# A two-layer model on one core: the first layer's prologue rearranged (first batch's convolutions among the row work, expert routing next, token sends beside the step sizes, order written out)

## The chip, the cores and the metric

The kernel runs on one core of one Trainium2 chip. A core has five engines that work at the same time, each through its own queue of instructions, strictly in order: TensorE (PE, matrix products and transposes; loading its weights shows as PEld), VectorE (DVE), ScalarE (ACT), GpSimd (POOL) and SyncE (SP, which only issues transfers). An engine that reaches an instruction whose inputs are not there waits, and everything behind it in its queue waits too. The metric is device time of one execution in microseconds; the times given are medians of several executions, and the profile is of one further execution.

## What is computed

Two layers over 8 batches of 512 tokens of width 256. Each layer is `x = x + attention(norm(x)) + experts(norm(x))`. In the first layer, which the change touches, "attention" is a state-space scan and "experts" a routed feed-forward net:

```python
xn = _layernorm(x)
# scan: in two directions, 8 heads, chunks of 128 tokens
zxbcdt = xn @ in_proj_w.T                     # z | x,B,C | dt
xBC = silu(causal_conv(xBC, conv_w, 4 taps))
dt = softplus(dt + dt_bias);  A = -exp(A_log)
Y = ssd(x * dt, A * dt, B, C, chunk=128)      # forward and backward direction
y = shift(Y + x * D); y = y_fw + y_bw + x * (x @ fc_D_w.T + D)
out = rmsnorm(y * silu(z)) @ out_proj_w.T
# experts: each token goes to the one expert of highest probability
probs = softmax(xn @ Wr + br); gate, idx = max(probs), argmax(probs)
y = gate * (relu(xn @ W1[idx] + b1[idx]) @ W2[idx] + b2[idx])
```

The second layer is softmax attention with 16 heads and a top-2 routed net of seven experts. Its code is the same in both kernels.

## The kernel before

**Stages of the first layer.** (1) *Row work*, `norm_and_project`: for each of the 8 batches, mean and variance (lines 134, 135), a Newton reciprocal root (164 to 174), the normalised rows `xn` (140), their transpose `xT` (147, 148), and a small product that gives 16 step-size inputs and 8 expert scores per token (`pp`, 152, copied to `proj`, 156). `xT` is also written to memory (`xtd`, 366) for later. (2) *Step sizes* in `steps()`: the softplus as a series in VectorE instructions (392 to 406), from which `dt` and `da` come. (3) *The first batch's convolutions*: for each of eight channel blocks a product `pj` (746) from `xT` and `w_in`, an ACT instruction that starts `cv` (755), three taps on VectorE (759), a tanh on ACT (763) and one more VectorE instruction (764). (4) *The opening*: decays, the first chunk's segment sums, the skip term (`skip`, 782 to 791; `start`, 809 and 816), the exponent rows for all chunks (`edges`). (5) *The chunk loop*: 64 chunks, eight per batch (four positions, two directions). Chunk n's matrix `mt` is multiplied by the masked `cb` (`weigh`, 970) and used in `inside` (`yd`, 976), then come `before` (`yoff`, 994), `behind` (`sp`, 1002) and the segment sums of the chunk after (`seg`, 938). In between are pieces of the neighbouring batches' convolutions and outputs.

**What fills the loop.** Each chunk calls `fill(1)` four times (five times for the first two of a batch; two more calls through `fill(2)` in the last eight chunks). A fill advances one generator by one step: first `route0()` (softmax, arg-max, ranks, slot numbers `slot0`, then 32 sends of token rows to their expert slots `xd0` with GpSimd's indirect transfers, line 459, two per step), then `blocks()` (39 blocks of 128 slots through the experts: gathers of weights, line 524; `xdT_ps` 540, `h_ps` 559, `y_ps` 577), and when both are used up `late()` (per batch: add the experts' rows, second normalisation, transpose, router product; lines 628 to 666). Block 0 reads `xd0`, so it waits for all 32 sends. `late` for a batch waits until the scan's output of that batch is done.

**Who sets the order.** Stages 1 to 4 stand outside the written-out region: there a planner places the instructions of each engine by its own estimates. From the chunk loop on (`tc.manual_schedule`) the program order is the order of every queue.

**Transfers of the prologue.** The slots `xd0` are first cleared with zeros from ACT's queue (`clear`, line 121, one eighth per batch). A batch's rows `u` are loaded through two buffers, so the load for batch b waits until the rows of batch b-2 are normalised.

Of the kernel before, what the change touches and what calls it, by code (L numbers as in the profile page):

```python
# [17 lines left out]
P = 128  # L18
# [35 lines left out]
def bc(ap, axis, shape):  # L54

    return ap.unsqueeze(axis).to_broadcast(shape)
# [3 lines left out]
def tile_kernel(ctx: ExitStack, tc: tile.TileContext, t, out: bass.AP):  # L60
# [63 lines left out]
        )  # L124


    def norm_and_project(x_of, xn, xT_of, w_proj, n_proj, proj, pool, bank):

        for b in range(B):
            x = x_of(b)  # L130
            mv = pool.tile([P, TPB, 2], FP, name="mv", tag="mv")
            for c in range(TPB):
                st = pool.tile([P, 6], FP, name="st", tag="st", bufs=4)
                V.bn_stats(st, x[:, c, :])
                V.bn_aggr(mv[:, c, :], st)
            ve = pool.tile([P, TPB], FP, name="ve", tag="ve")
            V.tensor_scalar(ve, mv[:, :, 1], EPS, None, ALU.add)
            rs = rsqrt(pool, ve, [P, TPB])
            for c in range(TPB):
                V.tensor_scalar(  # L140
                    xn[:, b * TPB + c, :], x[:, c, :], mv[:, c, 0:1], rs[:, c : c + 1], ALU.subtract, ALU.mult
                )
            xT = xT_of(b)
            for k in range(KC):
                tp = bank("tp", [P, S], 0)
                for c in range(TPB):
                    T.transpose(tp[:, c * P : (c + 1) * P], xn[:, b * TPB + c, k * P : (k + 1) * P], ident)
                A.copy(xT[:, k, :], tp)
            pp = bank("pp", [P, TPB, n_proj], 1)
            for c in range(TPB):  # L150
                for k in range(KC):
                    T.matmul(
                        pp[:, c, :], xT[:, k, c * P : (c + 1) * P], w_proj[:, k, :],
                        start=(k == 0), stop=(k == KC - 1),
                    )
            V.tensor_copy(proj[:, b * TPB : (b + 1) * TPB, :], pp)

    def rsqrt(pool, v, shape):

# [199 lines left out]
    proj = r0b.tile([P, NTILE, 2 * NH + NE], FP, name="proj0", tag="proj0")  # L359

    def steps():
        pool, big = r0p, r0b
        xTs = {}

        def keep(b):
            Y.dma_start(out=xtd[b], in_=xTs[b])

        def x_of(b):
            if b:
                keep(b - 1)  # L370
            if b >= 2:
                ask(b)

            n = NBLK // B + 1
            clear(xd0, NBLK * P, b * n, min(NBLK, (b + 1) * n))
            if b == 3:
                Y.dma_start(out=w_in, in_=t["w_in"])
            if b == 5:
                Y.dma_start(out=w_out, in_=t["w_out"])
            return us[b]  # L380

        def xT_of(b):
            xTs[b] = m2.tile([P, KC, S], FP, name="xT", tag="xT")
            return xTs[b]

        norm_and_project(x_of, xn, xT_of, w_small, 2 * NH + NE, proj, pool, bank)
        keep(B - 1)

        v, u, z, z2 = (row(n).rearrange("p (t e) -> p t e", e=2 * NH) for n in ("sp_v", "sp_u", "sp_z", "sp_z2"))
# [12 lines left out]
        V.tensor_tensor(acc, acc, z, ALU.mult)  # L404
        V.tensor_scalar(acc, acc, 2.0, None, ALU.mult)
        V.scalar_tensor_tensor(dt.rearrange(f2), v.rearrange(f2), 0.0, acc.rearrange(f2), ALU.max, ALU.add)
        ea = big.tile([P, 2 * NH], FP, name="ea", tag="ea")
        A.activation(ea, a_log, AF.Exp)
        V.tensor_scalar(ea, ea, -1.0, None, ALU.mult)
        for d in range(2):  # L410
            of = slice(d * NH, (d + 1) * NH)
            V.tensor_tensor(da[:, d], dt[:, :, of], bc(ea[:, of], 1, [P, NTILE, NH]), ALU.mult)


    def route0():

        big = r0b

# [23 lines left out]
        V.tensor_copy(slot0, slots_of(big, oh, rank, "a"))  # L442
# [12 lines left out]
        yield  # L455

        sent = []
        for i in range(NTILE):
            one = G.indirect_dma_start(
                out=xd0, out_offset=bass.IndirectOffsetOnAxis(ap=slot0[:, i : i + 1], axis=0),  # L460
                in_=xn[:, i, :], in_offset=None, bounds_check=NBLK * P - 1, oob_is_err=False,
            )
            for other in sent:
                tc.declare_no_dep(one.ins, other.ins, reason="rows go to slots of their own")
            sent.append(one)
            if i % 2:
                yield

    def decays():
# [26 lines left out]
        A.activation(e8, ct, AF.Exp)  # L496
        Y.dma_start(out=exd.rearrange("g p l -> p g l"), in_=e8)

    steps()
    l1c = tl = w_r = rb = w_q = w_o = w_uk = w_uv = w_kv = band = slot1 = iota_n = proj1 = vt0 = qk0 = r1b = noop = None  # L500
    tls = ExitStack()
    for k in range(HC):
        V.tensor_scalar(w_out[:, k, :], w_out[:, k, :], norm_w[:, k : k + 1], None, ALU.mult)

    with ExitStack() as es:
        p1, p2, psum = m1, m2, mp
        H3 = [P, NH, P]
# [518 lines left out]


        first = batch[0]
        first.load()
# [12 lines left out]
        decays()  # L1042
        chunk[0].prepare()
        chunk[0].segments()
        chunk[0].cross(range(NH))
        chunk[1].prepare()
        chunk[0].pairs(first)
        chunk[0].weigh()
        edges()
        batch[1].load()  # L1050
        e2 = None

        with tc.manual_schedule(engines=ENGINES):

            def others(n):

# [36 lines left out]
            for n in range(N):  # L1093
# [683 lines left out]
```

## Time and profile before

| what | us |
|---|---|
| median of 3 runs (2068.0 to 2072.36) | 2070.32 |
| the profiled execution, its own time | 2064.15 |
| its span | 2062.4 |
| first chunk's `yd` | 130.72 |
| slot numbers ready, first send | 148.4, 148.90 |
| last send starts | 203.71 |
| first block's first product | 213.02 |
| last chunk's `yd` | 1061.81 |
| last output product of the scan ends | 1095.7 |

PE is busy 1838.8 us (89% of the span), VectorE 1435.8 (70%), ACT 1178.1 (57%), GpSimd 627.8 (30%). A timeline line gives the start and the length in us, the engine, the line of the kernel, the operation, what it writes and reads, and how many instructions are merged in it; a bracket gives the idle time of the engine before it and what ended it. A line of the table by stretches gives the stretch, its length, and then busy time and (in brackets) instruction count of PE, PEld, VectorE, ACT and GpSimd, the TensorE clock granted (1.00 is full), the share of the DMA engines' time and the rate.

### The profile page before, as it was taken

What the parts mean: (1) busy time and instruction counts of PE and PEld (TensorE: products, weight loads), DVE (VectorE), ACT (ScalarE), POOL (GpSimd) and SP (SyncE); (2) the same over time, 40 slices, a digit from 0 to 9 for tenths busy, and PEclk for the clock granted to TensorE, in tenths of its full rate; (3) what the DMA queues carried; (4) which work ended last, traced back from release to release, by engine and by line L of the source; (5) the groups of instructions that cost most, each with busy time, mean ns of one, the idle gap of its engine ahead of it and who ended that gap; (6) DMA issues with size and microseconds to landing.
All of it is one profiled execution on the core that took longest, in us unless ns stands there. A gap on an engine that the chain in (4) does not pass through costs nothing. (4 is left out here: it accounts for less than half of the span.)

```text
span 2062.4 us, 33308 instructions
## 1 busy us (share of the span) xinstructions
PE 1838.8 (89%) x11760; PEld 1235.9 (60%) x11760; DVE 1435.8 (70%) x3311; ACT 1178.1 (57%) x2536; POOL 627.8 (30%) x572
## 2 busy tenths in 40 slices
PE   5666999999999999987776998899999999999987
PEld 5333676767677677744544544466666666666654
DVE  4684766667485665668665787567777877787785
ACT  2243454545354454545433667577777877787776
POOL 0048644546454454555430035300000000000030
PEclk9877999999999999998776899799999999999998
DMA  7113654655455465543542254322231221213170
GB/s 265 62 49 113 212 196 159 210 186 194 148 186 196 156 218 187 159 130 101 169 138 96 98 183 150 108 80 72 68 93 45 87 72 55 81 54 104 34 162 14
DMA packets 150439, 262.34 MB, mean 127 GB/s; under 512 B 22361, under 2 KB 107212, under 8 KB 138368
## 3 DMA queue, kind: packets, MB, share of 16 engines
q1 hardware_dynamic: 112288, 139.62, 21.1%
q0 software_dynamic: 28512, 110.92, 17.3%
q10 hardware_dynamic: 9472, 9.67, 1.4%
q8 instruction: 93, 1.52, 0.3%
q14 instruction: 74, 0.61, 0.1%
HBM read 188.46 MB, written 76.68 MB: 129 GB/s over the span
## 5 line engine op out<-in xcount | busy, mean ns | idle before, releaser
L1476 DVE TENSOR_SCALAR s<-s_ps 128x512 f32<-128x512 f32 x512 | 318.1, 683 | 200.4 <-PE s_ps L1471 178.6
L1486 ACT ACTIVATE s<-s,ng 128x512 f32<-128x512 f32 x512 | 351.1, 727 | 14.7 <-DVE ng L1482 13.3
L1478 DVE CUSTOM_DVE_ANT_0 s<-s,band 128x512 f32<-128x512 f32 x512 | 323.0, 687 | 0.0
L1493 PE MATMUL p_ps<-ident,s 128*128 128x128 f32 x2048 | 291.7, 283 | 33.2 <-ACT pT L1494 33.2
L1494 ACT COPY pT<-p_ps 128x512 f32<-128x512 f32 x512 | 280.4, 590 | 44.6 <-PE p_ps L1493 35.5
L1493 PEld LDWEIGHTS p_ps<-ident,s 128*128 128x128 f32 x2048 | 242.6, 145 | 101.5 <-ACT pT L1494 59.8
L1281 POOL DMA_INDIRECT x<-e_yo,e_to x28 | 43.4, 1552 | 605.4 <-ACT e_yo L1280 542.6
L746 PE MATMUL pj<-xT,w_in 128*128 128x512 f32 x384 | 206.1, 664 | 14.9 <-DVE cv L759 12.2
L1471 PE MATMUL s_ps<-kT,qT 16*128 16x512 f32 x1024 | 164.6, 678 | 14.0 <-DVE s L1476 9.5
L559 PEld LDWEIGHTS h_ps<-xdT,w 128*128 128x128 f32 x1248 | 149.4, 193 | 22.3 <-issue 21.5
L559 PE MATMUL h_ps<-xdT,w 128*128 128x128 f32 x1248 | 153.0, 276 | 2.9 <-DMA w<-in_w_dram,w_idx 2.9
L759 DVE SCALAR_TENSOR_TENSOR cv<-pj,w_conv_w,cv 128x511 f32<-128x511 f32 (+2 forms) x192 | 143.1, 746 | 9.7 <-ACT cv L755 5.7
L577 PE MATMUL y_ps<-w,hT 128*128 128x256 f32 x624 | 147.3, 380 | 0.0
L922 POOL TENSOR_TENSOR au<-da,half 128x512 f32<-128x512 f32 x64 | 78.6, 1229 | 221.5 <-PE seg L938 119.8
L1502 PE MATMUL o_ps<-pT,vt 128*32 128x256 f32 x2048 | 139.9, 403 | 1.8 <-issue 1.7
L577 PEld LDWEIGHTS y_ps<-w,hT 128*128 128x128 f32 x624 | 115.9, 190 | 32.1 <-issue 18.1
L746 PEld LDWEIGHTS pj<-xT,w_in 128*128 128x128 f32 x384 | 72.7, 207 | 98.6 <-issue 89.6
L996 POOL TENSOR_TENSOR yT<-yT,ex 128x512 f32<-128x512 f32 (+1 forms) x48 | 59.2, 1233 | 226.1 <-DVE ex L995 159.2
L1262 PE MATMUL e_hp<-e_xdT,e_w 128*128 128x256 f32 x448 | 122.3, 395 | 2.2 <-ACT e_xdT L1247 0.8
L1502 PEld LDWEIGHTS o_ps<-pT,vt 128*32 128x32 f32 x2048 | 66.4, 115 | 94.1 <-issue 62.9
L1275 PE MATMUL e_yp<-e_w,e_hT 128*128 128x256 f32 x448 | 118.9, 388 | 0.1
L951 ACT ACTIVATE mt<-seg,mid 64x64 f32<-64x64 f32 x512 | 109.5, 309 | 0.8
(296 smaller groups left out, 3019.8 us busy)
## 6 DMA issues: line engine op xcount, KB each, us to landing
ex<-exd SPq DMA_DIRECT2D x96, 128.0 KB
u<-in_u_dram SPq DMA_DIRECT2D x16, 512.0 KB
xtd<-xT SPq DMA_DIRECT2D x16, 512.0 KB
fr<-fdd SPq DMA_DIRECT2D x64, 128.0 KB
xT<-xtd SPq DMA_DIRECT2D x15, 512.0 KB
od<-os SPq DMA_DIRECT2D x28, 256.0 KB
e_w<-in_ei_dram SPq DMA_DIRECT2D x7, 1024.0 KB
e_w<-in_eo_dram SPq DMA_DIRECT2D x7, 1024.0 KB
```

Source lines behind the costliest of these rows:

```text
L559: T.matmul(hp[:, i, :], w1[:, k * FF + f * P : k * FF + (f + 1) * P], xdT[:, k * P : (k + 1) * P], start=(k == 0), stop=(k == KC - 1),)
L577: T.matmul(yp, hT[f // 4][:, f % 4, :], w2[:, f * DM : (f + 1) * DM], start=(f == 0), stop=(f == FC - 1))
L746: T.matmul(pj, w_in[:, k, o * P : (o + 1) * P], self.xT[:, k, :], start=(k == 0), stop=(k == KC - 1))
L759: V.scalar_tensor_tensor(cv[:, s:], pj[:, : S - s], conv_w[:, q, 3 - s : 4 - s], cv[:, s:], ALU.mult, ALU.add)
L1262: T.matmul(hp, w1[:, k, f * P : (f + 1) * P], xdT[:, k, :], start=(k == 0), stop=(k == KC - 1))
L1471: T.matmul(sp[i], self.q[r, cols], self.k[r, :], start=True, stop=True)
L1476: V.tensor_scalar(self.p[i], sp[i], -CLAMP, CLAMP, ALU.max, ALU.min)
L1478: V.tensor_tensor_reduce(out=self.p[i], in0=self.p[i], in1=band[:, at : at + S], scale=1.0, scalar=-3.0e38, op0=ALU.mult, op1=ALU.max, acc ...
L1486: A.activation(self.p[i], self.p[i], AF.Exp, bias=self.ng[:, i : i + 1])
L1493: T.transpose(pp[:, k, :], self.p[i][:, k * P : (k + 1) * P], ident)
L1494: A.copy(pT[i][:, :, cc * P : (cc + 1) * P], pp)
L1502: T.matmul(op[32 * i : 32 * i + 32, half * 2 * P : (half + 1) * 2 * P], self.v[:, k, h * (AD + 1) : h * (AD + 1) + 32], pT[i][:, k, :], st ...
```

## The change

1. `first.x_part` and `first.bc_part` (the first batch's eight convolutions) are called from a new callback `behind(b)` after batch b's small product, two per batch from batch 2 on. Batch 0's `xT` gets a buffer of its own, and the load of `w_in` moves from batch 3 to batch 1.
2. The clears are no longer spread over the batches. After batch 4 a wide tile of zeros (`none`) is made on VectorE, from data of that batch, and four transfers from ACT's queue clear all of `xd0`, in runs of 4 KB.
3. The written-out region now begins before the routing. In it come, in this order: routing through `w_idx`, the skip term with the first 12 sends between its parts, the step sizes, tokens, decays, the first chunks' preparation, `edges`, segments, `start`, and `weigh`.
4. The softplus series takes one fused VectorE instruction per term in place of two.
5. The sends advance four per fill in place of two, and the last eight chunks fill once where they filled twice.

```diff
@@ def norm_and_project
             V.tensor_copy(proj[:, b * TPB : (b + 1) * TPB, :], pp)
+            behind(b)
@@ def steps
-            n = NBLK // B + 1
-            clear(xd0, NBLK * P, b * n, min(NBLK, (b + 1) * n))
-            if b == 3:
+            if b == 1:
                 Y.dma_start(out=w_in, in_=t["w_in"])
...
+        def behind(b):
+            for q in range(2 * b - 4, min(2 * b - 2, 2 * HC)) if b >= 2 else ():
+                part = first.x_part if q < HC else first.bc_part
+                slot(lambda: part(q % HC))
+            if b == B - 1:
+                while pending:
+                    slot()
+            if b == B // 2:
+                none = m1.tile([P, HC, S], FP, name="none", tag="z").rearrange("p k s -> p (k s)")[:, : TPB * DM]
+                V.tensor_scalar(
+                    none.rearrange("p (k d) -> p k d", d=DM), bc(zero[:, :DM], 1, [P, TPB, DM]),
+                    proj[:, b * TPB, :1], 0.0, ALU.min, ALU.max,
+                )
+                slots = xd0.rearrange("(p r) d -> p r d", p=P)
+                for lo in range(0, NBLK, 3 * TPB):
+                    n = min(3 * TPB, NBLK - lo)
+                    k = n // 3 if n % TPB else TPB
+                    A.dma_start(
+                        out=slots[:, lo : lo + n, :].rearrange("p (n k) d -> p n (k d)", k=k),
+                        in_=bc(none[:, : k * DM], 1, [P, n // k, k * DM]),
+                    )
@@ def step_sizes (was the end of steps)
-        V.tensor_scalar(acc, z2, 1.0 / 17.0, 1.0 / 15.0, ALU.mult, ALU.add)
-        for k in range(13, 0, -2):
-            V.tensor_tensor(acc, acc, z2, ALU.mult)
-            V.tensor_scalar(acc, acc, 1.0 / k, None, ALU.add)
-        V.tensor_tensor(acc, acc, z, ALU.mult)
+        V.tensor_scalar(acc, z2, 1.0 / 17.0, None, ALU.mult)
+        for k in range(15, 1, -2):
+            V.scalar_tensor_tensor(acc, acc, 1.0 / k, z2, ALU.add, ALU.mult)
+        V.scalar_tensor_tensor(acc, acc, 1.0, z, ALU.add, ALU.mult)
@@ def route0
-            if i % 2:
+            if i % 4 == 3:
                 yield
@@ before the chunk loop
-        first.load()
-        for q in range(4):
-            slot(lambda: first.x_part(q))
-        slot(), slot()
-        first.skip()()
-        first.ask(0), first.ask(1)
-        for q in range(4):
-            slot(lambda: first.bc_part(q))
-            if q == 0:
-                pending.append(first.start())
-        while pending:
-            slot()
-        first.tokens(0)(), first.tokens(3)()
-        decays()
-        chunk[0].prepare()
-        chunk[0].segments()
-        chunk[0].cross(range(NH))
-        chunk[1].prepare()
-        chunk[0].pairs(first)
-        chunk[0].weigh()
-        edges()
-        batch[1].load()
         with tc.manual_schedule(engines=ENGINES):
+            routing = route0()
+            for _ in range(6):
+                next(routing)
+            skip = first.skip()
+            next(routing)
+            skip()
+            next(routing)
+            first.ask(0), first.ask(1)
+            next(routing)
+            step_sizes()
+            for c in (0, TPB - 1):
+                first.tokens(c)()
+            decays()
+            chunk[0].prepare()
+            chunk[1].prepare()
+            edges()
+            chunk[0].segments()
+            chunk[0].pairs(first)
+            chunk[0].cross(range(NH))
+            pending.append(first.start())
+            while pending:
+                slot()
+            chunk[0].weigh()
+            batch[1].load()
...
-            rows, rest = itertools.chain(route0(), blocks()), late()
+            rows, rest = itertools.chain(routing, blocks()), late()
...
                 if n >= N - 8:
-                    fill(2)
+                    fill(1)
```

More of the change, by code (lines that the diff above doesn't have):

```diff
@@ L124, in clear, with norm_and_project @@
         )
-    def norm_and_project(x_of, xn, xT_of, w_proj, n_proj, proj, pool, bank):
+    def norm_and_project(x_of, xn, xT_of, w_proj, n_proj, proj, pool, bank, behind):
         for b in range(B):
@@ L361, in steps @@
     def steps():
-        pool, big = r0p, r0b
+        pool = r0p
         xTs = {}
@@ L382, in xT_of, with step_sizes @@
         def xT_of(b):
-            xTs[b] = m2.tile([P, KC, S], FP, name="xT", tag="xT")
+            if b == 0:
+                first.xT = xTs[b] = m2.tile([P, HC, S], FP, name="xT0", tag="yT")[:, :KC, :]
+            else:
+                xTs[b] = m2.tile([P, KC, S], FP, name="xT", tag="xT")
             return xTs[b]
-        norm_and_project(x_of, xn, xT_of, w_small, 2 * NH + NE, proj, pool, bank)
+        def behind(b):
[19 more added lines that the diff above has]
+                    )
+        norm_and_project(x_of, xn, xT_of, w_small, 2 * NH + NE, proj, pool, bank, behind)
         keep(B - 1)
+    def step_sizes():
+        big = r0b
         v, u, z, z2 = (row(n).rearrange("p (t e) -> p t e", e=2 * NH) for n in ("sp_v", "sp_u", "sp_z", "sp_z2"))
@@ L399, in steps @@
         acc = u
[L400 to L404 removed]
+        acc, z, z2, v = (a.rearrange(f2) for a in (u, z, z2, v))
+        V.tensor_scalar(acc, z2, 1.0 / 17.0, None, ALU.mult)
+        for k in range(15, 1, -2):
+            V.scalar_tensor_tensor(acc, acc, 1.0 / k, z2, ALU.add, ALU.mult)
+        V.scalar_tensor_tensor(acc, acc, 1.0, z, ALU.add, ALU.mult)
         V.tensor_scalar(acc, acc, 2.0, None, ALU.mult)
[L406 removed]
+        V.scalar_tensor_tensor(dt.rearrange(f2), v, 0.0, acc, ALU.max, ALU.add)
         ea = big.tile([P, 2 * NH], FP, name="ea", tag="ea")
@@ L497, in edges @@
         Y.dma_start(out=exd.rearrange("g p l -> p g l"), in_=e8)
-    steps()
     l1c = tl = w_r = rb = w_q = w_o = w_uk = w_uv = w_kv = band = slot1 = iota_n = proj1 = vt0 = qk0 = r1b = noop = None
     tls = ExitStack()
-    for k in range(HC):
-        V.tensor_scalar(w_out[:, k, :], w_out[:, k, :], norm_w[:, k : k + 1], None, ALU.mult)
     with ExitStack() as es:
@@ L1028, in tile_kernel @@
         first = batch[0]
+        steps()
         first.load()
-        for q in range(4):
-            slot(lambda: first.x_part(q))
-        slot(), slot()
-        first.skip()()
-        first.ask(0), first.ask(1)
-        for q in range(4):
-            slot(lambda: first.bc_part(q))
-            if q == 0:
-                pending.append(first.start())
-        while pending:
-            slot()
-        first.tokens(0)(), first.tokens(3)()
-        decays()
-        chunk[0].prepare()
-        chunk[0].segments()
-        chunk[0].cross(range(NH))
-        chunk[1].prepare()
-        chunk[0].pairs(first)
-        chunk[0].weigh()
-        edges()
-        batch[1].load()
+        for k in range(HC):
+            V.tensor_scalar(w_out[:, k, :], w_out[:, k, :], norm_w[:, k : k + 1], None, ALU.mult)
         e2 = None
         with tc.manual_schedule(engines=ENGINES):
+            routing = route0()
[22 more added lines that the diff above has]
+            batch[1].load()
             def others(n):
```

## The prediction

> **What bounds the kernel now.** First the busy time by stretches (span start, first `yd`, the first block, the last block, last output of the scan), then the timelines of single engines at these borders. Between them the layer falls into four parts.
>
> ```profile
> core 0: us, PE busy (x) PEld busy (x) DVE busy (x) ACT busy (x) POOL busy (x), PEclk, DMA share, GB/s
> 0.00:72.00 72.00, 44.51 (x190) 39.80 (x191) 33.76 (x162) 14.29 (x28) 3.30 (x20) 1.00 0.65 226
> ...
> 224.19:886.89 662.70, 649.63 (x3949) 469.31 (x3948) 436.98 (x731) 319.38 (x871) 338.08 (x293) 1.00 0.54 180
> 886.89:1095.70 208.81, 159.77 (x791) 102.13 (x790) 139.53 (x289) 89.04 (x204) 86.55 (x80) 0.82 0.42 132
> 130.72:224.19 93.47, 63.99 (x270) 35.27 (x270) 53.04 (x103) 29.70 (x79) 66.08 (x64) 0.79 0.38 129
> 72.90:130.72 57.82, 36.27 (x85) 13.50 (x84) 50.37 (x77) 24.28 (x50) 10.30 (x8) 0.78 0.11 35
> ```
>
> While blocks run beside chunks, 224.19 to 886.89 (45 chunks, 14.73 us each), PE is busy 98%: only work taken off PE would shorten that. Around it PE has gaps. In 72.9 to 130.7 VectorE is the bound (87%); in 130.7 to 224.2 six chunks run while routing and sends go by, without blocks; after 886.9 the blocks are used up and twelve chunks run beside `late`. So the change can win only by filling gaps outside the middle part, and what it moves out of one gap lands in another.
>
> ```profile
> 72.69 0.26 DVE L156 COPY proj<-pp 128x96 f32<-128x96 f32 x1 [5.33 <-PE pp L152]
> ...
> 148.41 0.18 DVE L442 CAST slot<-so_sa 128x32 int32<-128x32 f32 x1
> ```
>
> ```profile
> 148.90 1.24 POOL L459 DMA_INDIRECT xd<-xn,slot  x1 [6.92 <-DVE slot L442]
> ...
> 203.71 1.24 POOL L459 DMA_INDIRECT xd<-xn,slot  x1 [0.30 <-DMA xd<-xn,slot]
> 204.97 1.05 POOL L922 TENSOR_TENSOR au<-da,half 128x512 f32<-128x512 f32 x1
> 207.27 1.06 POOL L524 DMA_INDIRECT w<-in_w_dram,w_idx  x1 [1.25 <-DMA xd<-xn,slot]
> ```
>
> ```profile
> 130.72 1.98 PE L976 MATMUL yd<-mt,xdt 128*64 128x128 f32 x16 [4.19 <-DVE mt L970]
> ...
> 213.02 2.81 PE L559 MATMUL h_ps<-xdT,w 128*128 128x128 f32 x16 [2.87 <-DMA w<-in_w_dram,w_idx]
> ...
> 224.19 1.09 PE L976 MATMUL yd<-mt,xdt 128*64 128x128 f32 x16
> ```
>
> The reader sees that block 0 starts 8.1 us after the last send is done by GpSimd (204.95 to 213.02), and that it starts in chunk 5.
>
> **Row work with the convolutions in it: R = 96.5 instead of 72.9.** I walk the order in which the changed kernel issues on each engine, with the rows' lengths. Eight transposes take 2.1 us, sixteen small products 3.7, a convolution's product 1.98 (four records, clock 1.00) or 3.75 (cold, at 85.09), its ACT parts 0.78 and 0.63, its taps 2.3, its last VectorE part 0.6; a batch's statistics 1.8, its normalisation 1.35. Batches 0 and 1 now go through PE back to back: 10.2 to 22.3. First product to 24.3, ACT to 25.1, taps to 27.4; statistics of batches 2 and 3 to 31.0 (their `u` is issued behind two `xtd` writes, at 19.4, and lands in time); one last part, six taps, two Newton roots and two normalisations with another last part: 40.2. Here VectorE's queue holds the copy of batch 2's `proj` and then batch 3's. PE does transposes 2, half a convolution, products 2 (to 43.5), transposes 3, the other half, products 3 (to 50.0), so VectorE waits some 7 us between them. Three taps more, the root and batch 4's normalisation: 57.8; two taps and a last part: 60.5; wait for products 4: 63.4; the wide zero tile (1.0, twice the 0.43 of a 512-wide TENSOR_SCALAR), taps, batch 5: 69.6; batch 6's statistics and three scalings of `w_out`: 71.6. Batch 7's `u` can be asked only at 69.7, when the clears (5 MB at the 381 GB/s of the stretch 14 to 22 us, 13 us from 66) are moving. Before, `u` of batch 2 took 8 us through such traffic (issued 14.6, used 22.5); so it lands at 77.3, its statistics end at 79.2, and 7.3 us of queue follow plus 9.7 for transposes, products and copies of 6 and 7: R = 96.5. With no such delay it is 92; if that load took twice as long, 104.
>
> [...]
>
> **From R to the first block.** Routing on VectorE, by its rows from 73.59 to 74.92 and from 130.49 to 149.83, with PE's `both` (2.07) and an ACT exp (0.5) inside and what lies between left out: 16.3 to `slot0`, 1.3 more to `w_idx`. Before, these were shared with the first two chunks; now PE has only small products beside them. The first send goes at R + 16.6 = 113.1 against 148.9. Sends cost 1.28 each (150.44 and 158.72 on), so twelve end at R + 32. The step sizes take 15.8 (ACT 1.35, the reciprocal 3.39, eight fused instructions at 0.72, six others and `da`): `da` at R + 33.4. The fusing saves seven TENSOR_SCALAR of 0.42, 2.9 us, which are in this sum. Then GpSimd: four `xdt` (1.05 each), one `au` 1.1: R + 37.8; `seg` 1.1; the masked `cb` on VectorE at R + 39.8. `start` stands in front of `weigh` in VectorE's queue: 4 x (0.6 + 1.4) = 8.0, then `weigh` 1.5: first `yd` at R + 49.5 = 146, 15 us later than before. (In the old trace `start` was spread among the taps.)
>
> All other sends stand in chunk 0's five fills: 5 x 4 = 20. Queued on GpSimd: four sends (R + 47.5 to 52.6), two `xdt` that need `xp` behind the first `yd` (to 55), four sends (60.1), `xdd` (61.2), twelve sends (76.6). Behind them stand `au` and the weight gathers, and in PE's queue block 0's transpose stands in chunk 1, before that chunk's `cb`, `sp` and next `seg`. With the old 8.1 us, block 0 starts at R + 84.7 = 181, and chunk 2's `yd` follows 9 us later (two times 2 us of `h_ps`, `sp`, `seg`, half a `y_ps`, transposes): R + 94 = 190.5. So the chunk loop stands still some 20 us in chunk 1, with nothing beside it.
>
> **Middle and end.** Blocks start 32 us earlier (213 to 181), but in chunk 1 and not 5. The pattern of pieces is the same, shifted by four chunks: 45 chunks at 14.73, 662.7 us, bounded by PE. Then 16 chunks instead of 12 share the same `late` steps (seven batches inside, one left over in both). What does a chunk without block or `late` cost? The old end shows 11.98 between two `yd` (904.01 to 915.99), and 10.7 and 12.0 in other light ones. Going through the 16 chunks with old chunks of like content gives 252 for this part instead of 208.8, so 43 for four chunks. Bounds: 34 (8.5 each, if spreading `late` thinner hides some of it) to 50. The fill taken from the last eight chunks is in this: batch 6's `late` moves from the tail into chunk 62.
>
> Sum for the changed kernel: 96.5 + 94 + 662.7 + 251.8 + the unchanged 966.7 (2062.4 - 1095.7; order and pieces of the second layer are the same) = 2071.7 against 2062.4: +9.3. The profiled execution took 2064.15, the median of the runs is 6.2 above it; I carry the difference over: 2070.3 + 9.3 = 2079.6, predicted 2080. In short: change = R - 130.2 + (four chunks at the end) = 96.5 - 130.2 + 43.
>
> **Rivals.** (a) *Faster*: the row work hides the convolutions. Old PE and VectorE are busy only 44.5 and 33.8 of 72 us, and the convolutions bring PE 16 and VectorE 23, so room is there. It decides at R = 83 (below: faster by over 0.2%). That needs the waits at `proj` copies 2 and 3 (7 us) and batch 7's late load (4.5) to vanish together with little else. For R = 80 the time is 2063. Against it: those copies are in front of ready taps in an in-order queue. (b) *Parity*: R = 92 and 39 for the last four chunks: +1, 2071. For it: the old end has 49 us of PE gaps. (c) *The first block is later still*: PE stays cold after a 20 us stall (the clock is 0.79 there in the old stretch), VectorE's `start` doubles beside GpSimd (at 124.16 two such took 2.97 instead of 1.53), the load of `u` doubles: +10 to +20 more, 2095. (d) *It does nothing*: routing was hidden beside the first chunks, the new order only permutes. The four unmatched chunks speak against it; it falls in with (b).
>
> **How the numbers follow.** Forecast 0.55, its own range 2074 to 2089; (a) 0.16; (b) with (d) 0.16; (c) 0.13. The range takes (b), most of (a) and the lower part of (c): 2063 to 2095. Less than 0.2% (4 us) can't be told from no change by these runs. Faster 0.17, same 0.16, slower 0.67.
>
> **What would show it.** Last `proj` copy near 96; first send near 113; first `yd` near 146; a gap of some 20 us on PE in chunk 1 that ends with the gather of weights, first `h_ps` near 181; last `h_ps` some 34 us earlier than 876, and about 252 us from chunk 47's `yd` to the last output product. It is wrong if the row work ends before 85, if the sends don't hold the first block, or if the last four chunks cost much less than 10 us each.

## The result, and the profile after

The changed kernel takes 2106.2 us (median; 2098.4 to 2110.6) against 2071.3 of the kernel before on the same chip: ratio 1.0155, 95% interval 1.0122 to 1.0189; slower by some 32 us by that ratio, by 34.8 between the medians. The prediction was 2080 with a range up to 2095: the sign is right, the size is not.

Chunks are counted from 0. First the busy time by stretches of the changed kernel, cut as the old one was: last copy of `proj`, first `yd`, chunk 2's `yd` (from here on blocks run beside chunks), chunk 47's `yd` (blocks used up), chunk 52's `yd`, last output product. The columns are window, length, then busy time and instructions of each engine, TensorE's granted clock, DMA share and GB/s.

```profile
0.00:91.35 91.35, 54.63 (x224) 38.84 (x224) 52.81 (x195) 34.15 (x50) 3.48 (x21) 0.82 0.50 176
91.35:146.04 54.69, 18.15 (x56) 8.02 (x56) 41.93 (x80) 12.38 (x34) 28.56 (x26) 0.59 0.28 83
146.04:193.61 47.57, 22.85 (x109) 15.33 (x109) 11.34 (x18) 11.53 (x31) 30.27 (x30) 0.66 0.44 157
193.61:857.90 664.29, 649.93 (x3936) 467.96 (x3935) 436.76 (x727) 311.54 (x855) 335.94 (x288) 1.00 0.55 180
857.90:947.73 89.83, 62.51 (x290) 36.66 (x289) 49.48 (x86) 40.23 (x97) 36.59 (x35) 0.79 0.35 105
947.73:1129.83 182.10, 137.36 (x675) 88.64 (x674) 120.01 (x249) 74.40 (x174) 73.50 (x64) 0.79 0.35 110
```

The middle is what it was (45 chunks in 664.3 us, PE 98% busy). It starts 30.6 us earlier (193.6 against 224.2), and the part behind it is 271.9 us (89.8 + 182.1) instead of 208.8. So 63.1 lost at the end, 30.6 won at the start, 1.6 in the middle: the scan ends at 1129.8 instead of 1095.7, **34.1 later**. The medians differ by about as much (34.8). The 1.6 of the middle are no effect: in the twelve traces of this study that have 45 such chunks, with the same instructions in them, the middle takes 662.7 to 669.4.

The profiled execution (span 2108.9) shows 12.4 us more behind that point, 979.1 instead of 966.7. Nine other kernels of this study with the same second layer, on chips where the kernel before took 2067 to 2071, show 962.3 to 977.2 there, in no clear relation to their first layer; this term is spread between executions, of which more at the end.

The timelines of VectorE, GpSimd and PE at the borders, answering those of the old kernel:

```profile
73.09 0.75 DVE L134 BATCH_NORM_STATS2 st<-u 128x6 f32<-128x256 f32 x2 [8.88 <-DMA u<-in_u_dram]
```

```profile
107.97 1.22 POOL L487 DMA_INDIRECT xd<-xn,slot  x1 [103.64 <-DMA fr<-fdd]
...
173.10 0.97 POOL L487 DMA_INDIRECT xd<-xn,slot  x1 [0.30 <-DMA xd<-xn,slot]
174.07 1.08 POOL L946 TENSOR_TENSOR au<-da,half 128x512 f32<-128x512 f32 x1
176.38 1.06 POOL L548 DMA_INDIRECT w<-in_w_dram,w_idx  x1 [1.24 <-issue]
```

```profile
177.72 0.66 PE L564 MATMUL xdT_ps<-ident,xd 128*128 128x128 f32 x2 [20.21 <-DMA xd<-xd]
...
183.31 3.76 PE L583 MATMUL h_ps<-xdT,w 128*128 128x128 f32 x16 [4.50 <-DMA w<-in_w_dram,w_idx]
```

Batch 7's `u` holds VectorE 8.9 us, the sends go from 108 to 174, the 20 us stall of PE in chunk 1 stands in the trace, and block 0 starts at 183.3. Up to here everything is within some 5 us of the forecast. It is the end that isn't.

**Where the end goes.** Chunk 47 takes 26.2 us and chunk 49 24.6; the old end has no chunk above 21.1. Chunk 47 first: SyncE's queue, then VectorE and PE of the changed kernel, each from its timeline (SPq marks a transfer that SyncE issues; the second number is the time that the issue takes).

```profile
864.91 0.33 SPq L765 DMA_DIRECT2D xT<-xtd  x1
865.33 0.38 SPq L609 DMA_DIRECT2D yd<-yo  x1
869.01 0.33 SPq L72 DMA_DIRECT2D w_w_r<-in_w_r_dram  x1
...
874.12 0.43 SPq L730 DMA_DIRECT2D w_kt<-in_w_vt_dram  x1
```

```profile
877.62 0.69 DVE L736 TENSOR_TENSOR w_kt<-w_kt 128x512 f32<-128x512 f32 x1 [13.31 <-DMA w_kt<-in_w_vt_dram]
```

```profile
879.18 1.94 PE L741 MATMUL wp<-w_dn,w_kt 128*128 128x64 f32 x8 [14.19 <-DVE yT L840]
```

Read upwards: PE waits for VectorE, VectorE for `w_vt`, which SP asks for at 874.1; `w_vt` is the tenth of eleven loads of the second layer's weights, issued one after another from 869.0 on, behind the write of the last block's rows (their space comes free with it; SP waits 2.9 us for it), and that write stands in SP's queue behind the load of the next-but-one batch's `xT`, which goes out at 864.9. That load is issued in chunks with n % 8 = 7 alone, and 47 is such a chunk. In the old kernel the blocks ran out in chunk 51, which has no such load, and the same addition waited 4.0 us:

```profile
894.92 0.69 DVE L712 TENSOR_TENSOR w_kt<-w_kt 128x512 f32<-128x512 f32 x1 [3.99 <-DMA w_dn<-in_w_dn_dram]
```

Chunk 49 on VectorE and PE of the changed kernel:

```profile
891.46 0.47 DVE L652 SCALAR_TENSOR_TENSOR xr<-yg,gate,xr 128x256 f32<-128x256 f32 x1
...
894.20 0.48 DVE L652 SCALAR_TENSOR_TENSOR xr<-yg,gate,xr 128x256 f32<-128x256 f32 x1 [1.59 <-DMA yg<-yd,slot]
...
900.11 2.31 DVE L783 SCALAR_TENSOR_TENSOR cv<-pj,w_conv_w,cv 128x511 f32<-128x511 f32 x3
```

```profile
902.56 1.93 PE L892 MATMUL ss<-z,ones 128*32 128x512 f32 x8 [7.42 <-DVE cv L783]
```

The sums and statistics of batch 0's rows for the second layer (L652 to L660), which wait for gathered rows, stand from 891.5 to 899.6 in front of the taps of the next batch's convolution, and PE's `ss` waits for those taps. In the old kernel the first of these row steps came after chunk 51, and most of them in the last eight chunks, which carry no convolution.

### The profile page after: what moved, and what is told of

Same layout as the page of the kernel before. It is cut to its first block, busy times and chain, and to the rows that moved or that the text cites. A ratio compares the mean times of both kernels' runs of the same rounds, so it can differ in the third digit from the quotient of the medians.

```text
span 2108.9 us, 33301 instructions
## 1 busy us (share of the span) xinstructions
PE 1834.1 (87%) x11760; PEld 1232.1 (58%) x11760; DVE 1434.1 (68%) x3305; ACT 1185.6 (56%) x2542; POOL 630.9 (30%) x572
## 4 chain that ended last, share of the span: by engine, by line
PE 36%; ACT 6%; DVE 5%; issue 2%; DMA 1%; another core or an unknown queue 1%; POOL 1%; ACTq 0%; SPq 0%; DVEq 0%; POOLq 0%
PE p_ps L1523 8%; PE s_ps L1501 6%; PE o_ps L1532 6%; PE e_yp L1305 5%; PE e_hp L1292 4%; ACT s L1516 3%; ACT pT L1524 2%; DVE s L1508 1%; DVE s L1506 1%; PE qp L255 1%; PE fin L1464 1%; PE vp L270 1%; PE kp L263 1%; PE op L920 1%
## 5 line engine op out<-in xcount | busy, mean ns | idle before, releaser
L1524 ACT COPY pT<-p_ps 128x512 f32<-128x512 f32 x512 | 280.1, 589 | 45.3 <-PE p_ps L1523 34.9
L770 PE MATMUL pj<-xT,w_in 128*128 128x512 f32 x384 | 198.5, 642 | 17.7 <-DVE cv L783 10.4
L583 PEld LDWEIGHTS h_ps<-xdT,w 128*128 128x128 f32 x1248 | 152.1, 196 | 25.8 <-issue 24.8
L783 DVE SCALAR_TENSOR_TENSOR cv<-pj,w_conv_w,cv 128x509 f32<-128x509 f32 (+2 forms) x192 | 142.9, 745 | 8.0 <-ACT cv L779 3.9
L601 PEld LDWEIGHTS y_ps<-w,hT 128*128 128x128 f32 x624 | 115.8, 190 | 32.7 <-issue 18.3
L770 PEld LDWEIGHTS pj<-xT,w_in 128*128 128x128 f32 x384 | 69.7, 200 | 94.6 <-issue 78.6
L1532 PEld LDWEIGHTS o_ps<-pT,vt 128*32 128x32 f32 x2048 | 67.1, 116 | 93.7 <-issue 63.1
L946 POOL TENSOR_TENSOR au<-da,half 128x512 f32<-128x512 f32 x64 | 80.6, 1260 | 129.8 <-PE seg L962 124.5
```

Source lines behind the costliest of these rows:

```text
L583: T.matmul(hp[:, i, :], w1[:, k * FF + f * P : k * FF + (f + 1) * P], xdT[:, k * P : (k + 1) * P], start=(k == 0), stop=(k == KC - 1),)
L601: T.matmul(yp, hT[f // 4][:, f % 4, :], w2[:, f * DM : (f + 1) * DM], start=(f == 0), stop=(f == FC - 1))
L770: T.matmul(pj, w_in[:, k, o * P : (o + 1) * P], self.xT[:, k, :], start=(k == 0), stop=(k == KC - 1))
L1524: A.copy(pT[i][:, :, cc * P : (cc + 1) * P], pp)
L1532: T.matmul(op[32 * i : 32 * i + 32, half * 2 * P : (half + 1) * 2 * P], self.v[:, k, h * (AD + 1) : h * (AD + 1) + 32], pT[i][:, k, :], st ...
```

## The experiments

**Theory A**, formed from these traces: the end's additional 20 us (63 instead of the forecast 43) come from where the second layer's row steps (`late`) stand, part A1 the queue of SP in chunk 47, part A2 their meeting with taps in chunks that still carry convolutions. **Rival B**: four chunks more cost 16 us each whatever stands in them. **Rival C**: the loss lies ahead of the chunks. Each kernel is the changed one with the edit shown, unless said otherwise.

**The two extra fills back**

```diff
                 if n >= N - 8:
-                    fill(1)
+                    fill(2)
```

> The changed kernel with two extra fills in each of the last eight chunks again, as before the change. Theory A (the end lost 20 us more than the four chunks because of where the steps of the second layer's rows stand: they now fall into chunks that still carry convolutions, and the second weights are asked behind a held load): these eight steps come earlier into chunks 56 to 63, which have no convolutions; the end part of 271.9 us becomes some 5 us shorter, time about 2101. Rival B (a chunk without blocks costs some 16 us whatever stands in it): no change, 2106. Rival C (the loss lies ahead of the chunks): no change, 2106.

2104.5 us, ratio 1.0174 [1.0138, 1.021]; end part 274.6 us. The fill moves nothing that can be measured; A's 5 us for it fail.

**`late` held until chunk 51**

```diff
+            n_of = [0]
             def fill(n):
                 for _ in range(n):
-                    if next(rows, "end") == "end":
+                    if next(rows, "end") == "end" and n_of[0] >= 51:
                         next(rest, None)
...
             for n in range(N):
+                n_of[0] = n
...
                 if n >= N - 8:
-                    fill(1)
+                    fill(2)
```

> The changed kernel with the second layer's row steps held back until chunk 51, where they began before, and the two extra fills: chunks 47 to 50 then carry neither blocks nor these steps. Theory A: chunks 47 to 50 take 8.5 to 12 us each (43 together), chunks 51 to the end as before the change (208.8), so the end part is 252 instead of 271.9 and the time about 2086. Rival B: chunks 47 to 50 still take some 16 each, end part 270, time 2105. Rival C: as B, the time does not move.

2077.1 us, ratio 1.0044 [1.0025, 1.0064]. The end part is 249.1 us; chunks 47 to 50 take 11.5, 10.35, 9.7 and 10.1, 41.7 together. The stretch of this kernel that answers 857.90 to 947.73 of the changed one:

```profile
861.83:916.78 54.95, 43.00 (x233) 24.71 (x232) 43.85 (x62) 33.13 (x85) 30.33 (x28) 0.94 0.33 92
```

Holding work back makes the kernel faster by 1.1% (1.0044 against 1.0155, some 23 us), and the end part shorter by 22.8 us: 34.9 us less up to chunk 52, 12.1 more behind it. The scan ends only 18.9 us earlier, at 1111.0, since the middle took 668.5 us in this execution. In the stretch shown PE is busy 78% instead of 70%, and its granted clock is 0.94 instead of 0.79. B is out: a chunk with neither blocks nor `late` costs 10.4 us. The remainder, +0.4%, is left for C.

**Held until chunk 48 only**

```diff
-                    if next(rows, "end") == "end":
+                    if next(rows, "end") == "end" and n_of[0] >= 48:
```

(with the counter and the two fills as above)

> The changed kernel with the second layer's row steps held back until chunk 48 (not 51), with the two extra fills: they still fall into chunks that carry convolutions, but the second weights are asked one chunk after the load of the batch after next, not behind it in SP's queue. Theory A1 (the jam in SP's queue is the larger part): chunk 47 takes 11.5 instead of 26, the rest of the end as in the changed kernel or a little less; end part 255 to 260, time 2085 to 2092. Theory A2 (the larger part is VectorE, where row steps and taps meet in the chunks with convolutions): the end part stays at 265 or more, time 2098 to 2104.

2087.2 us, ratio 1.009 [1.0059, 1.0121], end part 253.9. One chunk of delay brings 20.7 of the 25.5 us that separate `late` from 47 (274.6, with the same fills) and from 51 (249.1). By its expectation this would be A1, the queue. The chunks say otherwise: 47 and 48 together take 28.7 us here and 33.8 with `late` from 47, which is 5 us; chunks 49 to 51 take 41.3 instead of 55.4, which is 14. Chunk 49 still holds the taps of two convolutions and two of the four row sums; but here the first taps stand in front (894.5), and the sums behind them (896.9 to 898.9) find their rows there and wait for nothing. The other two sums come in chunk 50. The time was as A1 had it, for a reason nearer to A2: not that row sums and taps share a chunk, but that sums which wait stand ahead of the taps.

**One load moved behind the fills**

```diff
                 else:
-                    if b + 2 < B:
-                        batch[b + 2].load()
                     put(next_, "tokens", 0), put(next_, "tokens", 3), put(now, "z_part", 3)
...
+                if n % 8 == 7 and n // 8 + 2 < B:
+                    batch[n // 8 + 2].load()
                 if n % 8 < 2:
                     fill(1)
```

> The changed kernel with one line moved: the load of the next-but-one batch's xT is asked at the end of its chunk, behind the fills, not at the start. Theory A1 (in chunk 47 this load waits in SP's queue for its buffer, the last blocks' write and the second weights stand behind it, and VectorE and PE wait for the weights): the wait of 13.3 us of VectorE for w_vt goes, chunk 47 takes 12 to 15 instead of 26.2, time 2092 to 2096. Rival (the weights are late because they are twelve loads asked in one chunk, whatever stands ahead): chunk 47 stays at 24 to 26, time 2104 to 2106.

This and two later kernels ran on a chip on which the kernel before took 2040.4 us, so ratios count: 1.0126 [1.0096, 1.0156], against 1.0155 [1.0122, 1.0189] of the changed kernel; the intervals overlap, so only the trace tells. The end part is 260.9 us, chunk 47 takes 20.3. VectorE's timeline of this kernel:

```profile
874.03 0.69 DVE L736 TENSOR_TENSOR w_kt<-w_kt 128x512 f32<-128x512 f32 x1 [8.17 <-DMA w_kt<-in_w_vt_dram]
```

The wait goes from 13.3 to 8.2 us and not away: both sides were half right. Five to six microseconds of chunk 47 are the load in the queue; the rest are the loads themselves (eleven by the trace), asked in the chunk in which VectorE's queue comes to the sum of two of them. In this kernel SP issues the first at 865.4, as VectorE's wait begins, and `w_vt` at 870.6; it is there at 874.0. So some 5 us go into issuing one load after another and 3 into the transfer. No run spread the loads out.

**`late` skipped in chunk 49 alone**

```diff
-                    if next(rows, "end") == "end":
+                    if next(rows, "end") == "end" and n_of[0] != 49:
```

> The changed kernel with the second layer's row steps skipped in chunk 49 alone (they go on in chunk 50). In the changed kernel chunk 49 took 24.6 us: VectorE's queue held batch 0's sums, waiting for gathered rows, ahead of the taps of two convolutions, and PE waited 7.4 us. Theory A2 (the meeting of these steps with taps in one chunk costs, not the steps as such): chunk 49 takes 10 to 12, chunks 50 and 51 grow by less than what 49 gives, the three chunks 49 to 51 together 42 to 48 instead of 55.8, ratio to the kernel before some 0.005 lower, 1.010. Rival (the steps bring their cost with them wherever they stand): the three chunks together stay at 53 to 58, ratio 1.0155 as the changed kernel.

2097.8 us, ratio 1.0136 [1.009, 1.0182]; by the times alone it can't be told from the changed kernel. By the trace chunks 49 to 51 take 12.8 + 15.1 + 19.8 = 47.7 us instead of 55.8, and the end part is 264.9 instead of 271.9: A2's figure. Chunk 49 gives 11.7 us, chunks 50 and 51 take 3.6 more, and of the 8 us 7 stay won at the end of the scan.

The end parts side by side, all between starts of `yd` and the end of the last output product, each from one execution:

| kernel | chunks 47 to 51 | chunk 52 to the end | end part |
|---|---|---|---|
| changed | 89.8 | 182.1 | 271.9 |
| two extra fills | 89.2 | 185.4 | 274.6 |
| load moved | 83.0 | 177.9 | 260.9 |
| `late` not in 49 | 80.8 | 184.1 | 264.9 |
| `late` from 48 (and fills) | 70.0 | 183.9 | 253.9 |
| `late` from 51 (and fills) | 55.0 | 194.2 | 249.1 |

**The row work alone.** Routing and sends go back into the chunks' fills, two sends a fill, and the two extra fills are back.

```diff
-            if i % 4 == 3:
+            if i % 2:
                 yield
...
             routing = route0()
-            for _ in range(6):
-                next(routing)
+            step_sizes()
             skip = first.skip()
-            next(routing)
             skip()
-            next(routing)
             first.ask(0), first.ask(1)
-            next(routing)
-            step_sizes()
+            pending.append(first.start())
+            while pending:
+                slot()
             first.tokens(0)(), first.tokens(TPB - 1)()
             decays()
...
```

> The changed row work alone: convolutions among the rows, the wide clears, the fused step sizes; routing and sends go back into the chunks' fills (two sends a fill), block 0 starts in chunk 5, the two extra fills are back. R (last copy of proj) stays at 91.4. Theory A (row work pays: what it costs ahead of R comes back behind it, since the convolutions' 23 us of VectorE are gone from a stretch where VectorE was busy 87%): da 17 us behind R, first yd at 124 to 130, six chunks of 93.5 in all, chunk 6's yd at 217 to 223, end part 209 as before the change; time 2062 to 2068. Rival C (the stretch behind R is a chain of waits across engines, not VectorE's sum, so the 18 us lost ahead of R come back only in part): first yd at 138 or later, chunk 6's yd at 232, time 2077 or more.

2065.5 us, ratio 0.9997 [0.9981, 1.0014]: no difference from the kernel before. The stretches from R to the first `yd` and on to chunk 6's:

```profile
91.30:126.32 35.02, 15.99 (x44) 7.25 (x45) 30.51 (x37) 9.52 (x24) 10.14 (x8) 0.60 0.18 47
126.32:222.27 95.95, 63.13 (x271) 34.37 (x270) 54.00 (x103) 32.20 (x90) 65.80 (x64) 0.82 0.38 130
```

R is 18.4 us later than in the old kernel, the first `yd` 4.4 us earlier: VectorE is 87% busy from R to the first `yd` here as it was before; the stretch is 22.8 us shorter, and VectorE's busy time in it 19.9 us less (30.5 instead of 50.4), so what left it comes back. Of the 4.4, 1.9 remain at chunk 6, and the end part (212.0) takes them. So C is out for the row work: it is neutral, and **everything that the change loses it loses by moving routing and sends** (with the order of the opening that goes with it and, through them, the blocks).

**One send a fill behind the first twelve**

```diff
-            if i % 4 == 3:
+            if i >= 11 or i % 4 == 3:
                 yield
```

> The changed kernel with one send a fill behind the first twelve, so that the twenty others reach into chunk 4 and block 0 starts in chunk 5 as before the change. Theory A: no 20 us stall of PE in chunk 1; first yd still at 146; six light chunks of 10.7 to 12 us, so chunk 6's yd comes at 210 to 218 (before the change 224.2); middle 663, end part 209; time 2056 to 2065, faster than before the change. Rival B: the end part is 209 too, but the six chunks take 16 each, chunk 6's yd is at 242, time 2088. Rival C: the row work and routing up to the first yd cost what they cost and the sends still hold the chunks, 2080 or more.

2080.0 us, ratio 1.0053 [1.0037, 1.0068]. The end part is 213.5, as A and B both had it, and the stall of PE in chunk 1 is gone; but the first six chunks take 83.7 us, 14 each, not 11, and the first `yd` is at 148.7. C's figure is met. A's figure for a light chunk was taken from the end of the scan, where GpSimd sends nothing. That the sends are what makes the early chunks dearer is not shown: chunks 0 and 1 take 8.5 and 10.3 us, though six sends run in chunk 1, and chunks 2 to 5 take 14.8 to 19.1. Routing ahead of the chunks costs 22.3 us up to the first `yd` (148.7 against 126.3 with the row work alone) and returns 12.2 in the six chunks.

**Eight empty fills ahead of the blocks**

```diff
-            rows, rest = itertools.chain(routing, blocks()), late()
+            rows, rest = itertools.chain(routing, range(8), blocks()), late()
```

(`late` from chunk 49, two extra fills)

> The changed kernel with eight empty fills between the last send and the blocks, so that block 0 starts in chunk 3 instead of 1, and with the second layer's row steps held until chunk 49, two extra fills. Theory: PE no longer stands still in chunk 1 waiting for block 0's rows; chunk 2's yd at 165 to 177, chunk 4's yd at 195 (in the changed kernel chunk 2's yd was at 193.6), so two chunks less are left for the end: end part from chunk 49's yd 230, time 2060 to 2068, some 15 less than with the steps held to 51 alone. Rival (the sends hold the chunk loop through GpSimd whether blocks are there or not): chunk 2's yd at 185 or later, time 2077 as with the hold alone.

Ratio 1.0108 [1.0079, 1.0137] on the chip with 2040.4. PE's timeline:

```profile
175.96 2.08 PE L962 MATMUL seg<-au,row_lt 64*128 64x512 f32 x4 [15.56 <-POOL au L946]
```

With no block in chunk 1, PE stands still there all the same, for `au`, which GpSimd makes behind the sends. Chunk 2's `yd` is at 178.0, 15.6 us before the changed kernel's and within 1 us of the theory's range; chunk 4's is at 204.0 instead of the 195 expected. The scan ends at 1113.1, no earlier than with the hold to chunk 51 alone (1111.0), whose ratio of 1.0044 is lower. The rival's 185 for chunk 2 is not met either, but what it names, sends that hold the loop, stands in the trace. The end part from chunk 49 is 244.3, not 230: `late` from 49 is dear again.

**The row work alone, with four sends a fill**

```diff
-            if i % 2:
+            if i % 4 == 3:
                 yield
```

(against the kernel with the row work alone; `late` from chunk 49)

> The row work alone, but with four sends a fill, so that block 0 starts in chunk 3 instead of 5, and with the second layer's row steps held until chunk 49. Theory (what the early blocks win at the start they keep only if the chunks given up there were dear and the ones added at the end are light): chunks of 15.6 us at the start are exchanged for chunks 49 and 50 of some 10.3 at the end; two such exchanges are worth 10 us if the sends are not in the way, 5 if GpSimd's queue (32 sends, 41 us) delays chunks 1 to 3: first yd at 126, chunk 4's yd at 187 to 196, end part from chunk 49's yd 230, time 2054 to 2062. Rival: the sends stop the chunk loop as in the changed kernel (20 us), time 2070 or more.

Ratio 1.0187 [1.0157, 1.0218], the highest of all, though its interval overlaps that of the changed kernel. Chunk 2 takes 33.9 us, in which PE waits 18.3 us for `mt`, and the end part from chunk 49 is 252.3 us. Four sends a fill stop the chunk loop also when it starts from the old order. The exchange of dear first chunks for light last ones, which had looked like 5 to 10 us, does not pay in either form.

**The clears behind batch 6's rows**, in the changed kernel and with the row work alone:

```diff
-            if b == B // 2:
+            if b == B - 2:
```

> The changed kernel with the clears of the slots issued behind batch 6's rows instead of batch 4's, so that batch 7's load of u goes ahead of them. If the wait of 8.9 us for that load stands on the path: last copy of proj at 83 instead of 91.4, first send and first yd 8 us earlier, time about 2098. Rival: the clears now end after the first send could go (they take some 13 us from about 76), which gives back 0 to 5 of it: 2101 to 2106. Rival: the first yd waits for other work than the rows, no change.

> As the kernel with the row work alone, with the clears issued behind batch 6's rows. In the changed kernel that move took 8.9 us of wait away but brought only 1.5 at R, since PE's last three batches then went at half clock behind one another. If that holds here: R 89.8, first yd 1.5 to 2.2 earlier than in the kernel with the row work alone, time 2 less (no measurable difference). Rival: here PE has no other queue behind these rows and the full 8.9 come back: R 83, time 8 less.

2094.0 us (1.0141 [1.01, 1.0181]) in the first; 2068.3 (0.9995 [0.9977, 1.0014]) in the second: by the times neither can be told from the kernel it was made from. Batch 7's wait of 8.9 us is gone, but R is 89.8 and 89.3 instead of 91.4 and 91.3. ScalarE's, PE's and VectorE's timelines of the first show what took its place (ACTq marks transfers issued by ScalarE), and the window 74 to 91 PE's clock:

```profile
81.37 3.73 ACTq L406 DMA_DIRECT2D xd<-none  x4
85.22 1.07 ACT L148 COPY xT<-tp 128x512 f32<-128x512 f32 x2 [8.39 <-issue]
```

```profile
85.86 3.67 PE L152 MATMUL pp<-w_w_small,xT 128*128 128x24 f32 x16 [3.45 <-ACT xT L148]
```

```profile
89.56 0.26 DVE L156 COPY proj<-pp 128x96 f32<-128x96 f32 x1 [7.90 <-PE pp L152]
```

```profile
74.00:91.00 17.00, 10.70 (x46) 9.19 (x45) 5.47 (x18) 5.15 (x8) 0.00 (x0) 0.50 0.65 256
```

Two things took the place of the wait. The edit brought a delay of its own: the moved clears now stand in ScalarE's queue ahead of the copies of batch 7's `xT`, which ScalarE starts at 85.2, when the four are issued, and PE's products wait for these copies. And batches 6 and 7 go through PE at a granted clock of 0.50, with products of 3.67 us where batch 4 of the same kernel took 2.23. No run separates the two, so what the wait alone cost stays open.

**The fused step sizes alone, in the kernel before**

> The kernel before with the fused step sizes alone (seven TENSOR_SCALAR of 0.42 us less on VectorE). If VectorE is the bound there (busy 87% of 72.9 to 130.7 us): first yd 2 to 3 us earlier, at 128, and the time 2.5 less, 2066 to 2067. Rival (the chain passes elsewhere, or the chunks behind take it up): first yd or chunk 6's yd at the old place, no change.

2065.5 us, ratio 0.9996 [0.9981, 1.001]. The first `yd` is 0.9 us earlier (129.8), chunk 6's 0.3 later: no difference.

## Why the prediction was right or wrong

Point by point, forecast and profiled execution:

| step | predicted | measured |
|---|---|---|
| R, last copy of `proj` | 96.5 | 91.4 |
| batch 7's `u` used | 77.3 | 73.1 |
| first send | 113 | 108.0 |
| `da` | 130 | 125.6 |
| first `yd` | 146 | 146.0 |
| stall of PE in chunk 1 | 20 | 20.2 |
| first `h_ps` | 181 | 183.3 |
| chunk 2's `yd` | 190.5 | 193.6 |
| middle, 45 chunks | 662.7 | 664.3 |
| last `h_ps` | 842 | 849.0 |
| chunk 47's `yd` to the last output product | 251.8 | 271.9 |
| second layer | 966.7 | 979.1 (962 to 977 in the others) |

**Up to chunk 2** the walk holds, in part by luck: two errors cancel. Batch 7's load was used 4 us sooner, and R came 5 us sooner with it. Against that, from `da` to the first `yd` it took 20.5 us and not 16: `start` ran 12.0 us on VectorE (132.8 to 144.9) where 8.0 were in the sum. That is the part of rival (c) that was right. The late load, which rival (a) wanted gone, did not give back its 8.9 us in any run: the kernels with the clears moved have no such wait, and R came 1.5 to 2 us sooner, with the clears now in ScalarE's way.

**The clock** was read wrongly. The walk takes 2.1 us for eight transposes and 3.7 for sixteen small products, the lengths of the old row work, as those of a PE at full clock; the row of the old stretch from 0 to 72 us shows 1.00. PE of the kernel before, then of the changed one, show that the same instructions run in shorter times too:

```profile
53.22 3.67 PE L152 MATMUL pp<-w_w_small,xT 128*128 128x24 f32 x16 [0.51 <-ACT xT L148]
```

```profile
54.33 2.23 PE L152 MATMUL pp<-w_w_small,xT 128*128 128x24 f32 x16 [0.57 <-ACT xT L148]
...
79.78 2.10 PE L147 MATMUL tp<-ident,xn 128*128 128x128 f32 x8 [13.59 <-DVE xn L140]
```

Batches 2 to 5 of the changed kernel take 1.0 to 1.4 us for the transposes and 1.9 to 2.2 for the products (granted clock 0.85 from 24 to 74 us). Batches 6 and 7, behind 13.6 us of idle PE, take 2.1 and some 3.7 again, and there the granted clock is 0.50 (74 to 92 us), to the end, although PE is busy 11.0 of the last 12.4 us. The old row work has these slow lengths in all its batches, 1.9 to 2.1 and about 3.7, so the 1.00 of its row does not fit its own instructions. The same goes for batches 0 and 1 of the changed kernel (10 to 22 us, granted clock 1.00). Why the row shows it, no run here tells. The faster lengths, some 5 us less for batches 2 and 3 together, are also why PE was ahead of the walk: batch 3's products ended at 45.0 and not at 50.0, and batch 7's `u` was asked at 62.5 and not at 69.7, though it then took 10.5 us and not 7.6.

**The step that failed** is the end: "Going through the 16 chunks with old chunks of like content gives 252 for this part instead of 208.8, so 43 for four chunks", with 50 as the upper bound. It measured 271.9, 63 for four chunks. Half of the step is sound: four chunks with neither block nor `late` cost 41.7 us, and with `late` left at its old place the end part was 249.1. What failed is the assumption that `late`, begun four chunks earlier beside batches 5 and 6, costs what it cost beside batch 7 or less. It costs more: with `late` from 47 chunks 47 to 51 take 34.9 us longer, of which 12.1 come back behind them. The runs show: 5 to 6 us are one load ahead of the last block's write in SP's queue; about 8 go when chunk 49 alone is spared, 14 in chunks 49 to 51 when all begins one chunk later. What remains of the wait in chunk 47, 8.2 us with that load moved, is the issuing of eleven loads of weights one after another and the transfer of `w_vt`, whose use stands in VectorE's queue ahead of all else. These parts come from different runs and overlap, so they are not a sum.

**The rivals.** (a) fell at R and at the sends; (b) at the end. (c) named the longer `start`, but `start` was outweighed by the earlier R, and the time passed its 2095 by the end, of which (c) says nothing. (d), that the new order only permutes, fell too, but it holds for a large part of the diff: the row work does nothing (0.9997).

In sum for the first layer: +9.3 predicted, +34.1 measured; of the 24.8 between, 20.1 are the end, 3.1 the start, 1.6 the middle. The time missed the range's 2095 for this one term: less 20.1, 2106 is 2086.

## What to carry to other kernels

When a producer finishes earlier, its consumer starts earlier too, and meets different work: walk the consumer's steps through the new neighbours' queues (which loads stand ahead in the DMA queue, which engine has room) instead of pricing them by the old ones. In a pipeline bounded by one engine, as the middle is here by PE (98% busy), the gain from starting a stream earlier is only that dear chunks are exchanged for light ones at the other end; holding the low-priority stream back to its old place took 1.1 of the 1.55% away here. Moving a transfer out of one wait puts its issue into some engine's queue: look what stands behind it there. Here 8.9 us of waiting went, 1.5 to 2 were won, and ScalarE's copies stood behind the moved clears. And when a row of the profile says that a clock is full, hold it against the lengths of the same instructions elsewhere in the traces.

## What the runs showed of the hardware that was not expected

The second layer, the same instructions in the same order, took 962 to 979 us in eleven profiled executions (kernel before, changed kernel, nine of the study). Between the kernel before and the changed one, some 11 of the 12.4 us arise at one place, the second product of a projection ahead of attention. ScalarE of the changed kernel, and of the kernel before:

```profile
1247.92 0.60 ACT L256 ACTIVATE qc<-qp 128x512 f32<-128x512 f32 x1 [10.92 <-remote]
```

```profile
1210.83 0.60 ACT L255 ACTIVATE qc<-qp 128x512 f32<-128x512 f32 x1 [6.34 <-PE qp L254]
```

In the changed kernel PE had finished that product at 1240.6, yet ScalarE went on only 7.3 us later (its bracket says "remote", which names no engine of the core), and PE then worked at half clock (granted 0.50; 2.07 instead of 1.13 us for four matmuls) until about 1264. In the window 1238 to 1249 the DMA queue named "instruction" moved one packet; in the old kernel's window 1204 to 1215 it moved none. What ScalarE waited for is not shown; no run tried it.

One chip ran the kernel before in 2040.4 us instead of 2067 to 2071. By the traces of the three kernels run there, the first layer is no shorter than elsewhere; the second layer took 936 to 942 us, some 3% less than the 962 to 979 elsewhere, so the ratios here compare runs of one chip.
